# Seven products in place of eight block products for one side of a GRU gate, with VectorE adding partial sums onto a state tile

## The chip, the cores and the metric

The kernel runs on one core of a Trainium2 chip. A core has TensorE (PE, matrix products), VectorE (DVE), ScalarE (ACT), GpSimd (POOL) and SyncE (SP, which issues DMAs here). The engines run their own instruction queues and wait for one another by semaphores. [...] The metric is the device time of one execution in microseconds (us); lower is better.

## What is computed

The input is a batch of 128 graphs with 128 nodes and 256 features per node, and an integer adjacency matrix for each. Four graph layers follow one another, each with a residual and a layer norm: attention by edge type, a message layer, three steps of a gated graph network, and graph attention. The change lies in the third, whose core in the reference is:

```python
for i in range(3):
    m = einsum('bnd,de->bne', h, weight[i])
    aggr = einsum('bst,bsd->btd', A, m)          # A = (adj != 0)
    i_r, i_z, i_n = split(aggr @ w_ih.T + b_ih, 3)
    h_r, h_z, h_n = split(h @ w_hh.T + b_hh, 3)
    r, z = sigmoid(i_r + h_r), sigmoid(i_z + h_z)
    n = tanh(i_n + r * h_n)                      # the candidate
    h = (1 - z) * n + z * h
```

The kernel multiplies `weight[i]` and `w_ih` together once (`c_gi`), so that each step needs the aggregated state, `agT`, times `c_gi`, and the state, `hT`, times `w_hhT`. Everything is fp32, except the sums over neighbours, where the state is split in three bf16 parts.

## The kernel before

**Tiling.** Four graphs form a group, so a state is 256 features by 512 columns (4 graphs x 128 nodes), kept as two tiles of 128 x 512. There are 32 groups. Each passes through `loading`, `layer0`, `layer1`, `gru` and `layer3`; `gru` runs `step` three times. Work of several groups is on the chip at once: a group's three steps are spread over two periods (`SPAN = 2.0`), so the steps of two groups alternate.

**A gate by seven products.** A gate's product is a 256 x 256 weight times a 256 x 512 state, that is, 2 x 2 blocks of 128 x 128 weights and 128 x 256 states. Done directly it takes eight block products. `sums` (line 681) and `gate` (line 703) form it from seven, by Strassen's method in a form with few sums: `sums` adds blocks of the state into a tile (`t_h` for the hidden side, `t_m` for the aggregated side), and the weights' own combinations (`w_sh`, `w_sm`) are made once in `weights` (loop at line 382). In `gate` the four quarters of the result come out of two PSUM banks. The bank `shared` collects products 1, 6, 7 and 4 one after another, and after each of them its running sum is read out into a quarter of the result tile (`snapshot`, by the function `copied` or, at the end, `last`); the next product is added to the same bank only after that read. The bank `other` collects products 2, 5 and 3, and VectorE adds it to the quarters (`added`).

`gate` is called three times in a step:

- `q`: the hidden side of the candidate alone (seven products, one source), with ScalarE reading the shared bank and adding a bias (`hidden`);
- `t_r`: the reset gate, hidden and aggregated side together (fourteen products), ScalarE copying, and `tanh` at the end, since the sigmoid is computed as a tanh of half the argument;
- `t_z`: the update gate, likewise.

The aggregated side of the candidate isn't formed so. `direct` (line 667) takes two products of 512 columns for each half, four in all, into a bank of the tag `ps`. `candidate` (line 757) then computes on VectorE (t + 1) * q in place on the reset tile, adds the bank, and hands it to ScalarE's tanh.

**Buffers.** The PSUM tags `ps` and `gate` have four banks each. The result tiles `t_r`, `t_z`, `q` and the sums `t_m`, `t_h` have one buffer each.

**Order of the work.** Nothing is issued in the order of the program. Every operation is recorded, gets a due time (`nominal`) from `paced` (line 272), in units of `PERIOD`, and a list planner (line 971) issues, on each engine, that operation among those that can start which is due first. It reckons with costs per engine (`dve_cost`, line 249), with delays between engines (`HOP`, `PE_HOP`, `SLACK`) and with free buffers (`start_of`, line 948). It runs when the program is built, so that on the chip each engine has a fixed list. `M_START` and `M_END` set the due times of a step's aggregated part, in periods after the step's start (line 782).

**Layer 3** has a small negation of the softmax's reciprocal sums (`ninv`, line 875) on VectorE.

Of the kernel before, what the change touches and what calls it, by code (L numbers as in the profile page):

```python
# [13 lines left out]
OP = mybir.AluOpType  # L14
# [4 lines left out]
def kernel(  # L19
# [40 lines left out]
    P = 128  # L60
# [5 lines left out]
    NL = weight.shape[0]  # L66
# [69 lines left out]
    def tile_of(tag, shape, bufs=1, dtype=F32, pool=work):  # L136
        buf = Buf(pool, list(shape), dtype, tag, bufs)
        return View(buf, list(shape), [(0, n) for n in shape])

    def bank(tag="ps"):  # L140
        return tile_of(tag, [P, 512], 4, F32, psum)

    FAST = ("tensor_scalar", "tensor_scalar_add", "tensor_scalar_mul")
# [93 lines left out]


    LANDING = 4.2
    HOP = 0.235  # L240
    PE_HOP = 0.55
    SLACK = 0.873

    def pe_cost(op, n, sums):
# [2 lines left out]
    SPLIT = 0.056  # L247

    def dve_cost(op, n, sums):
        return 0.14 + n * (0.00056 if op in FAST else 0.00106)  # L250

    def act_cost(op, n, sums):
        return 0.6 if op == "dma_start" else 0.17 + n * 0.001 + (0.2 if sums else 0.0)
# [3 lines left out]

    PE = Engine("PE", nc.tensor, pe_cost)
    DVE = Engine("DVE", nc.vector, dve_cost)
    ACT = Engine("ACT", nc.scalar, act_cost)  # L260
    POOL = Engine("POOL", nc.gpsimd, pool_cost)
# [1 line left out]
    engines = (PE, DVE, ACT, POOL, SP)  # L263


    PERIOD = 82.744
    SPAN = 2.0
    EAGER, RUSH = 5.34, 0.516
    L0_START, L0_END, L1_START, L1_END, L3_START, L3_END = -2.032, -1.293, -0.75, -0.05, 0.173, 0.919
    H_END, M_START, M_END = 0.179, 0.179, 0.503  # L270

    def paced(start, end, pe_only=False):

# [2 lines left out]
        for op, t in zip(line, took):  # L276
            op.nominal = (start + (end - start) * sofar / total) * PERIOD
            op.urgent = pe_only
# [21 lines left out]
    w_hhT = tile_of("w_hhT", [P, KC, 3 * D])  # L300
    c_gi = tile_of("c_gi", [P, NL, KC, 3 * D])
# [1 line left out]
    w3x = tile_of("w3x", [P, KC, 2 + D])  # L303

    w_sh = tile_of("w_sh", [P, 3, 3, P])
    w_sm = tile_of("w_sm", [P, NL, 3, 2, P])

    def weights():

# [2 lines left out]
        for src, tag, bufs in ((w_ih, "hT", 6), (w_hh, "rest", 4)):  # L312
# [4 lines left out]
            if src is w_ih:  # L317
                for i in range(NL):
                    w = tile_of("hn", [P, KC, D], 3)
# [23 lines left out]
        for n, dst in enumerate((w_ihT, [w_hhT[:, c] for c in range(KC)])):  # L343
            for g in range(NGC // 2):
                nat = nats[n * NGC // 2 + g]
                ps = bank()
# [10 lines left out]
        for i in range(NL):  # L357
            wT = tile_of("h0T", [P, KC, D], 4)
            ps = bank()
# [7 lines left out]
            for d in range(KC):  # L367
                for n0, n1 in ((0, 512), (512, 3 * D)):
                    ps = bank()
                    with PE:  # L370
                        for e in range(KC):
# [4 lines left out]
                                start=(e == 0),  # L376
                                stop=(e == KC - 1),
# [2 lines left out]


        for n in range(NL + 1):
            by, gates = POOL if n > 1 else DVE, 3 if n == 0 else 2
            w = [
                (w_hhT[:, k] if n == 0 else c_gi[:, n - 1, k])[:, : 2 * gates * P].rearrange(
                    "p (g e x) -> p g e x", [P, gates, 2, P], g=gates, e=2
                )
                for k in range(KC)
            ]
            w_s = w_sh if n == 0 else w_sm[:, n - 1]  # L390
            a11, a12, a21, a22 = w[0][:, :, 0], w[1][:, :, 0], w[0][:, :, 1], w[1][:, :, 1]
            s2, s3, s4 = [w_s[:, j] for j in range(3)]
            by.tensor_sub(s3, a11, a21)
            by.tensor_add(a21, a21, a22)
            by.tensor_sub(s2, a21, a11)
            by.tensor_sub(s4, a12, s2)
# [8 lines left out]
        for c in range(KC):  # L405
            for h in range(2):
                DVE.scalar_tensor_tensor(
                    scr, w3x[:, c, 2:], 1.0, arow[:, h * D : (h + 1) * D],
                    op0=OP.mult, op1=OP.mult, accum_out=w3x[:, c, h : h + 1],
# [3 lines left out]
        ps = bank()  # L413
# [229 lines left out]
    def gru(g, s):  # L643
        hT = s.hT
        parts = s.parts
        R, Z, C = 0, KC, 2 * KC
        both = [0, 1]

        def step(i, hT, parts):
            agT, agps = [None] * KC, [None] * KC  # L650
# [13 lines left out]
                agT[c] = tile_of("agT", [P, T], 2)  # L664
                ACT.copy(agT[c], ps)

            def direct(w, v, q, ps=None, of=(0, 1), stop=True):

                start = ps is None
                ps = ps or bank("ps" if q >= C else "gate")  # L670
                with PE:
                    for k in of:
                        PE.matmul(
                            ps, w[:, k, q * P : (q + 1) * P], v[k],
                            start=(start and k == of[0]), stop=(stop and k == of[-1]),
                        )
                return ps

            H = T // 2

            def sums(by, v, w, w_s, src, tag):
# [18 lines left out]

                return of

            def gate(tag, q, sources, copied, added, last=None):

                t = tile_of(tag, [P, 4, H])
                shared, other = bank("gate"), bank("gate")

                def add(cols, p, first=False):  # L710
                    with PE:
                        for k, of in enumerate(sources):
                            PE.matmul(
                                cols, *of(q)[p], start=(first and k == 0),
                                stop=(p in (3, 4) and k == len(sources) - 1), skip_group_check=True,
                            )

                def snapshot(quarter):
                    copied(t[:, quarter], shared[:, :H], quarter // 2)
                    ops[-1].rush = RUSH  # L720

                add(shared[:, :H], 1, True)
                snapshot(0)
                add(other[:, :H], 2, True)
                add(shared[:, :H], 6)
                snapshot(1)
                add(other[:, H:], 5)
                add(shared[:, :H], 7)
                snapshot(3)
                added(t[:, 3], other[:, H:], t[:, 3])  # L730
                if last:
                    last(t[:, 3], t[:, 3], 1)
                add(shared[:, :H], 4)
                (last or copied)(t[:, 2], shared[:, :H], 1)
                add(other[:, H:], 3)
                halves = [t[:, 2 * c : 2 * c + 2].rearrange("p h n -> p (h n)") for c in range(KC)]
                added(halves[0], other, halves[0])
                if last:
                    last(halves[0], halves[0], 0)
                return halves  # L740
# [10 lines left out]
            def tanh(q):  # L751

                return lambda out, in_, c: ACT.activation(
                    out, in_, AF.Tanh, bias=brz[:, q + c : q + c + 1], scale=0.5
                )

            def candidate(c, ps, t, q):
                DVE.scalar_tensor_tensor(t, t, 1.0, q, op0=OP.add, op1=OP.mult)
                DVE.tensor_add(t, t, ps)
                n = tile_of("t_n", [P, T], 2)  # L760
                ACT.activation(n, t, AF.Tanh, bias=bih[:, 2 * KC + c : 2 * KC + c + 1], scale=1.0)
                d = tile_of("t_d", [P, T], 2)
                POOL.tensor_sub(d, hT[c], n)
                return n, d
# [18 lines left out]
            w_i = c_gi[:, i]  # L783
            of_h = sums(POOL, hT, w_hhT, w_sh, hT, "t_h")
            q0, q1 = gate("q", C, (of_h,), hidden, half_more)
            paced(at, at + H_END, True)
            aggregate(0)
            aggregate(1)
            paced(at + M_START - 0.03, at + M_START, True)
            of_m = sums(DVE, agT, w_i, w_sm[:, i], agps, "t_m")  # L790
            t0, t1 = gate("t_r", R, (of_h, of_m), copy, DVE.tensor_add, tanh(R))
            n1, d1 = candidate(1, direct(w_i, agT, C + 1), t1, q1)
            n0, d0 = candidate(0, direct(w_i, agT, C), t0, q0)
            z0, z1 = gate("t_z", Z, (of_h, of_m), copy, DVE.tensor_add, tanh(Z))
            update(1, z1, n1, d1)
            update(0, z0, n0, d0)
# [3 lines left out]
        for i in range(NL):  # L800
            hT, hn, parts = step(i, hT, parts)
# [9 lines left out]
    def layer3(g, s, first, last):  # L811


        n = last - first
# [4 lines left out]
        def tile(tag, shape, bufs=1):  # L819
            tag, bufs = names.get(tag, (tag, bufs))  # L820
            return tile_of(tag, shape, bufs)

        rT = []
        for c in range(KC):
            t = tile("rT", [P, n * N], 2)
# [11 lines left out]
        for b in range(n):  # L837
            ps = bank()
            with PE:
                for c in range(KC):  # L840
                    PE.matmul(
                        ps[:, : 2 + D], rT[c][:, b * N : (b + 1) * N], w3x[:, c, :],
                        start=(c == 0), stop=(c == KC - 1),
# [5 lines left out]
        e = f.rearrange("p (k b) c -> p b k c", [P, n, 4, 32], b=n)  # L849
        if end:  # L850
            ps = bank()
# [19 lines left out]
        pT, rinv = softmax(alpha, three, end, tile)  # L871
# [1 line left out]

        res = tile("xd", [P, n, D])
        ninv = tile_of(f"ninv_{three}", [P, n], 2)
        DVE.tensor_scalar_mul(ninv, rinv, -1.0)
        for h in range(n // 2):
            ps = bank()
            with PE:
# [3 lines left out]
            for j in range(2):  # L883
# [9 lines left out]
                op0=OP.add, op1=OP.add,  # L893
# [54 lines left out]
    def start_of(op):  # L948
# [4 lines left out]
        for buf in op.bufs:  # L953
            if buf.tile is None:
                slot = slot_at(buf)
                if slot is None:
                    return None
                at = max(at, slot + HOP)
                if buf.pool is psum:
# [11 lines left out]
    while left:  # L971
        best = None
        for e in engines:
# [5 lines left out]
            if best is None or at < best[0]:  # L979
                op = min(  # L980
                    (op for t, op in starts if t <= at),
                    key=lambda op: op.nominal - (EAGER if op.urgent and e is not PE else 0.0) - op.rush,
                )
                best = (at, op)
        at, op = best
        e = op.engine
# [12 lines left out]
        for other in op.after.values():  # L999
            other.waiting -= 1  # L1000
            hop = 0.0 if other.engine is e and not op.landing else SLACK if not other.urgent else HOP
            if hop == HOP and other.engine is PE:
                hop = PE_HOP
            other.ready = max(other.ready, end + hop)
# [31 lines left out]
```

## Time and profile before

| | |
|---|---|
| median of 3 runs | 2764.72 us (2764.5 to 2765.69) |
| profiled execution | 2763.69 us, its span 2761.8 us |
| mean granted TensorE clock | 0.991 |
| busy PE, DVE, POOL, ACT | 2702.3, 2304.1, 1666.2, 1584.2 us |
| DMA | 321.88 MB, mean 117 GB/s |

Every instruction is recorded by one helper, so all have one line (L232) and are told apart by their tiles: `gate<-t_m,c_gi` is a product of the aggregated side's sums with the combined weights into a bank of the tag `gate`, `ps<-agT,c_gi` a direct product of the candidate. PE is TensorE's products, PEld its weight loads. An fp32 product shows as two matmul instructions (x2). In a row of groups, the columns after the bar are busy time, mean ns of one, and the idle time before them with what ended it. In a row of waits they are total us, times, and the longest. In a timeline they are start and duration in us. Busy time of TensorE counts overlapped ends of matmuls, so that the distance between starts says more than durations.

### The profile page before, as it was taken

Reading aid. Unit: us, or ns where it says so; the run is one execution under the profiler, and the core shown is the slowest. Engines: PE = TensorE matmul, PEld = TensorE weight load, DVE = VectorE, ACT = ScalarE, POOL = GpSimd, SP = SyncE. Lnnn points to the kernel's source line nnn. Section 1 sums busy time; section 2 is a strip of 40 time slices with the busy share of each in tenths; the row PEclk is TensorE's granted clock in tenths of the full one; section 3 lists DMA queues with packets and bytes.
Section 4 is the critical chain, followed back from the end, with each engine's and each line's share of the span. In section 5 each row is a group of like instructions: output and inputs, shape, how many; then the busy total and the mean of one; then the engine's idle time right before and its main releaser. Section 6 shows DMA issues by size and latency. Waiting matters only on the chain.

```text
span 2761.8 us, 44048 instructions
## 1 busy us (share of the span) xinstructions
PE 2702.3 (98%) x13756; PEld 2138.1 (77%) x13756; DVE 2304.1 (83%) x5108; ACT 1584.2 (57%) x3704; POOL 1666.2 (60%) x1606
## 2 busy tenths in 40 slices
PE   8899999999999999999999999999999999999996
PEld 5677787887887887887887887887887887787774
DVE  5787888888888888888888888888888898888875
ACT  4454665555665655665655665655665655665554
POOL 4544666655666655666655666655676655675542
PEclk9999999999999999999999999999999999999996
DMA  5545555555555556555655556655556555545441
GB/s 121 129 90 99 115 126 129 120 109 124 122 125 131 121 108 129 118 124 133 121 107 127 121 121 134 121 110 123 121 121 134 124 109 120 116 110 118 99 88 43
DMA packets 1397130, 321.88 MB, mean 117 GB/s; under 512 B 1142560, under 2 KB 1388448, under 8 KB 1396896
## 3 DMA queue, kind: packets, MB, share of 16 engines
q1 hardware_dynamic: 1394448, 316.69, 53.7%
q10 hardware_dynamic: 2448, 2.36, 0.3%
q8 instruction: 111, 1.82, 0.3%
q14 instruction: 123, 1.01, 0.1%
HBM read 185.74 MB, written 133.15 MB: 115 GB/s over the span
## 4 chain that ended last, share of the span: by engine, by line
PE 94%; DVE 3%; POOL 1%; ACT 1%; DMA 1%; issue 1%; ACTq 0%; POOLq 0%; DVEq 0%; SPq 0%
PE gate L232 52%; PE ps L232 42%; DVE t_r L232 0%; POOL t_h L232 0%; DVE xb L232 0%; DVE st L232 0%; DMA rest<-in_L_gnn_w_hh_dram 0%; DVE z L232 0%; POOL rstd L232 0%; DMA hn<-in_L_gnn_weight_dram 0%; POOL xa L232 0%; DVE xa L232 0%; DVE t_d L232 0%; POOL t_d L232 0%; DVE hT L232 0%
## 5 line engine op out<-in xcount | busy, mean ns | idle before, releaser
L232 ACT ACTIVATE q<-gate,bhn 128x256 f32<-128x256 f32 x384 | 183.0, 477 | 314.4 <-PE gate L232 313.1
L232 PE MATMUL ps<-agT,c_gi 128*128 128x512 f32 x768 | 356.0, 592 | 0.0
L232 PE MATMUL gate<-t_h,w_hhT 128*128 128x256 f32 x1152 | 345.2, 381 | 5.7 <-ACT t_z L232 4.3
L232 PE MATMUL gate<-t_h,w_sh 128*128 128x256 f32 x1152 | 337.1, 383 | 4.2 <-ACT q L232 1.7
L232 POOL TENSOR_TENSOR rstd<-rstd,neg_half 128x4 f32<-128x4 f32 (+1 forms) x128 | 142.4, 1112 | 218.2 <-DVE rstd L232 215.1
L232 PEld LDWEIGHTS gate<-t_h,w_sh 128*128 128x128 f32 x1152 | 213.7, 191 | 62.8 <-issue 30.4
L232 PEld LDWEIGHTS ps<-xs,xT 128*128 128x128 f32 x2048 | 249.7, 193 | 11.5 <-ACT xs L232 2.6
L232 PEld LDWEIGHTS gate<-t_h,w_hhT 128*128 128x128 f32 x1152 | 211.7, 191 | 56.1 <-issue 16.3
L232 PE MATMUL ps<-xs,xT 128*128 128x128 f32 x2048 | 251.8, 276 | 2.2 <-ACT xs L232 1.3
L232 ACT COPY t_z<-gate 128x256 f32<-128x256 f32 x288 | 107.1, 372 | 244.6 <-PE gate L232 244.0
L232 PE MATMUL ps<-w_um,x1T 128*128 128x512 f32 x512 | 237.1, 595 | 0.2 <-ACT x1T L232 0.2
L232 PEld LDWEIGHTS ps<-agT,c_gi 128*128 128x128 f32 x768 | 145.8, 190 | 114.5 <-issue 106.0
L232 PE MATMUL gate<-agT,c_gi 128*128 128x256 f32 x768 | 229.2, 380 | 2.6 <-ACT agT L232 2.6
L232 PE MATMUL gate<-t_m,c_gi 128*128 128x256 f32 x768 | 228.5, 379 | 0.0
L232 PE MATMUL gate<-t_m,w_sm 128*128 128x256 f32 x768 | 228.4, 379 | 0.0
L232 PE MATMUL gate<-hT,w_hhT 128*128 128x256 f32 x768 | 222.8, 385 | 5.6 <-DVE hT L232 5.6
L232 POOL TENSOR_SCALAR mk<-a_f 128x512 uint8<-128x512 f32 x128 | 201.3, 1579 | 12.2 <-DVE alpha L232 6.6
L232 ACT ACTIVATE xs<-xT,acol 128x512 f32<-128x512 f32 x256 | 182.1, 717 | 40.9 <-PE ps L232 31.5
L232 POOL MEMSET hu<- 128x1 f32 x128 | 10.3, 96 | 303.8 <-DVE fac L232 224.5
L232 DVE TENSOR_TENSOR t_z<-gate,t_z 128x256 f32<-128x256 f32 x192 | 104.2, 543 | 101.4 <-ACT t_z L232 53.7
L232 POOL TENSOR_TENSOR t_d<-h0T,t_n 128x512 f32<-128x512 f32 x64 | 82.9, 1295 | 174.0 <-ACT t_n L232 171.1
L232 PEld LDWEIGHTS gate<-hT,w_hhT 128*128 128x128 f32 x768 | 141.8, 191 | 48.1 <-issue 23.6
(197 smaller groups left out, 7280.1 us busy)
## 6 DMA issues: line engine op xcount, KB each, us to landing
way_h<-z SPq DMA_DIRECT2D x190, 256.0 KB, 2.4
hn<-way_h SPq DMA_DIRECT2D x760, 64.0 KB, 2.4
way<-z SPq DMA_DIRECT2D x126, 256.0 KB, 3.2
x_blocks<-in_x_dram SPq DMA_DIRECT2D x256, 64.0 KB, 2.3
x_in<-in_x_dram SPq DMA_DIRECT2D x32, 512.0 KB, 3.8
way_x<-xb SPq DMA_DIRECT2D x32, 512.0 KB, 2.9
way_p<-z SPq DMA_DIRECT2D x62, 256.0 KB, 2.6
probT<-way_p SPq DMA_DIRECT2D x248, 64.0 KB, 2.3
```

Of the source, the lines that this page charges most:

```text
L232: getattr(self.engine, name)(*[a.real() if isinstance(a, View) else a for a in args], **{k: a.real() if isinstance(a, View) else a for k, ...
```

## The change

The aggregated side of the candidate goes through `gate` as a fourth call. It has one source (`of_m`), and in place of copies it has `onto`: VectorE adds the shared bank's running sum onto the quarter of the reset tile, which by then holds (t + 1) * q. There is no result tile of its own: `whole` turns the reset gate's half back into a view of its whole buffer. `direct` goes. Both (t + 1) * q operations are recorded ahead of the gate, first half first. The weight combinations are made for three gates in place of two for `c_gi` too (`w_sm` grows), and `ninv` goes to ScalarE. The planner's costs, delays, period and due times are changed.

```diff
-    HOP = 0.235
-    PE_HOP = 0.55
+    HOP = 0.217
+    PE_HOP = 0.441
...
-        return 0.14 + n * (0.00056 if op in FAST else 0.00106)
+        return 0.095 + n * (0.00056 if op in FAST else 0.00106) + (0.08 if sums else 0.0)
...
-    PERIOD = 82.744
+    PERIOD = 82.004
...
-    L0_START, L0_END, L1_START, L1_END, L3_START, L3_END = -2.032, -1.293, -0.75, -0.05, 0.173, 0.919
-    H_END, M_START, M_END = 0.179, 0.179, 0.503
+    L0_START, L0_END, L1_START, L1_END, L3_START, L3_END = -1.947, -1.293, -0.7, -0.05, 0.168, 0.874
+    H_END, M_START, M_END = 0.179, 0.12, 0.503
...
-    w_sm = tile_of("w_sm", [P, NL, 3, 2, P])
+    w_sm = tile_of("w_sm", [P, NL, 3, 3, P])
...
-            by, gates = POOL if n > 1 else DVE, 3 if n == 0 else 2
+            by = POOL if n > 1 else DVE
             w = [
-                (w_hhT[:, k] if n == 0 else c_gi[:, n - 1, k])[:, : 2 * gates * P].rearrange(
-                    "p (g e x) -> p g e x", [P, gates, 2, P], g=gates, e=2
+                (w_hhT[:, k] if n == 0 else c_gi[:, n - 1, k]).rearrange(
+                    "p (g e x) -> p g e x", [P, 3, 2, P], g=3, e=2
                 )
...
-            def direct(w, v, q, ps=None, of=(0, 1), stop=True):
...
+            def whole(t):
+                return View(t.buf, t.buf.shape, [(0, n) for n in t.buf.shape])
+
+            def onto(out, in_, c):
+                DVE.tensor_add(out, in_, out)
+
             def gate(tag, q, sources, copied, added, last=None):
...
-                t = tile_of(tag, [P, 4, H])
+                t = tile_of(tag, [P, 4, H]) if isinstance(tag, str) else whole(tag)
...
-                if last:
+                if last not in (None, onto):
                     last(t[:, 3], t[:, 3], 1)
                 add(shared[:, :H], 4)
                 (last or copied)(t[:, 2], shared[:, :H], 1)
                 add(other[:, H:], 3)
+                if copied is onto:
+                    added(t[:, :2].rearrange("p h n -> p (h n)"), other, t[:, :2].rearrange("p h n -> p (h n)"))
+                    return None
...
-            def candidate(c, ps, t, q):
-                DVE.scalar_tensor_tensor(t, t, 1.0, q, op0=OP.add, op1=OP.mult)
-                DVE.tensor_add(t, t, ps)
+            def candidate(c, t):
...
-            n1, d1 = candidate(1, direct(w_i, agT, C + 1), t1, q1)
-            n0, d0 = candidate(0, direct(w_i, agT, C), t0, q0)
+            for t, q in ((t0, q0), (t1, q1)):
+                DVE.scalar_tensor_tensor(t, t, 1.0, q, op0=OP.add, op1=OP.mult)
+            gate(t0, C, (of_m,), onto, DVE.tensor_add, onto)
+            n1, d1 = candidate(1, t1)
+            n0, d0 = candidate(0, t0)
...
-        DVE.tensor_scalar_mul(ninv, rinv, -1.0)
+        ACT.mul(ninv, rinv, -1.0)
```

More of the change, by code (lines that the diff above doesn't have):

```diff
@@ L665, in aggregate @@
                 ACT.copy(agT[c], ps)
-            def direct(w, v, q, ps=None, of=(0, 1), stop=True):
[L669 to L677, printed above, removed]
             H = T // 2
```

## The prediction

> **What bounds the kernel now.** I read the head of the page first, then the busy table over one period, then TensorE's waits.
>
> ```profile
> span 2761.8 us, 44048 instructions
> PE 2702.3 (98%) x13756; PEld 2138.1 (77%) x13756; DVE 2304.1 (83%) x5108; ACT 1584.2 (57%) x3704; POOL 1666.2 (60%) x1606
> PE 94%; DVE 3%; POOL 1%; ACT 1%; DMA 1%; issue 1%; ACTq 0%; POOLq 0%; DVEq 0%; SPq 0%
> ```
>
> TensorE (PE) is busy for 98% of the span, and 94% of the chain that ended last lies on it. The same POOL instruction on successive groups starts at 600.13, 682.79 and 765.47 us: a period of 82.67. The stretch table for one such period, 1400 to 1482.67 us, and TensorE's waits from 200 to 2500 us:
>
> ```profile
> core 0: us, PE busy (x) PEld busy (x) DVE busy (x) ACT busy (x) POOL busy (x), PEclk, DMA share, GB/s
> ...
> sum 82.67, PE 82.67 PEld 66.01 DVE 71.29 ACT 49.12 POOL 52.43; mean PE 27.56 PEld 22.00 DVE 23.76 ACT 16.37 POOL 17.48
> ```
>
> ```profile
> PE gate L232 <- POOL t_h L232: 0.8, 2, 0.6
> PE gate L232 <- ACT t_z L232: 0.5, 1, 0.5
> ```
>
> In 2300 us TensorE waited 1.3 us. VectorE (DVE) is next, 71.29 of 82.67 us (86%). Busy time of overlapped matmuls can flatter, so I take pitches (start to start) from the timeline of TensorE:
>
> ```profile
> 1430.01 0.59 PE L232 MATMUL gate<-hT,w_hhT 128*128 128x256 f32 x2
> ...
> 1433.03 0.59 PE L232 MATMUL gate<-t_m,w_sm 128*128 128x256 f32 x2
> ...
> 1451.87 3.60 PE L232 MATMUL ps<-agT,c_gi 128*128 128x512 f32 x8
> 1455.30 0.59 PE L232 MATMUL gate<-hT,w_hhT 128*128 128x256 f32 x2
> ```
>
> From 1430.01 to 1433.03 lie seven products of 256 columns: 3.02 us, 0.43 each. The candidate's four direct products of 512 columns take 1455.30 - 1451.87 = 3.43 us. There is no gap in either.
>
> [...] So each sum read out of an open bank is a round: product, read, next product. [...] The trace agrees on rounds (the waits above end with an evictor) and shows VectorE waiting for gate products. [...] the trace has 417 and 668, which I use.
>
> **The change, part by part.**
>
> *Products.* Per step 3.43 us goes and 7 x 0.43 = 3.02 comes: -0.41 us. Weight loads rise from 8 to 14 of 190 ns, two in each 0.43 us pitch, as the existing gates have them: hidden. Some 29 of the 32 periods lie where TensorE is full (200 to 2600 us), 87 of 96 steps: -35.7. The other nine I count half: -1.8. Sum -37.5 us.
>
> *VectorE.* The groups by shape:
>
> ```profile
> L232 DVE TENSOR_TENSOR t_r<-t_r,ps 128x512 f32<-128x512 f32 x192 | 131.4, 684 | 8.3 <-PE ps L232 0.6 <-PE gate L232 0.5
> L232 DVE TENSOR_TENSOR t_z<-gate,t_z 128x512 f32<-128x512 f32 x96 | 64.2, 668 | 47.6 <-PE gate L232 47.5
> L232 DVE TENSOR_TENSOR t_z<-gate,t_z 128x256 f32<-128x256 f32 x96 | 40.1, 417 | 53.7 <-ACT t_z L232 53.7
> ```
>
> Two adds of 684 ns go; five of 417 and one of 668 come: 2.75 - 1.37 = +1.39 us a step, +4.2 a period. The negation of rinv leaves VectorE (median 665 ns, once a group). So 71.29 + 4.2 - 0.7 = 74.8 of about 82 us: 91%. That costs nothing by itself while TensorE has 81 us to do. Were that cover gone, every microsecond of it would lengthen the period.
>
> *Rounds.* The candidate gains four rounds a step on its shared bank (384 in all), with one product each, so other work must fill them. The hidden-side gate already runs this shape with ScalarE as reader, and all gates already have one VectorE read between two products of `other`; TensorE's 1.3 us above is what they cost. Uncovered rounds elsewhere stop TensorE for 0.46, 0.51, 0.56 us (around 2590 to 2720 us). Bounds: none uncovered, 0; every one, 384 x 0.5 = 192 us. I choose one in twenty, 19 x 0.5 = +9.6 us, because VectorE's queue is fuller than ScalarE's (57%) and because work in the `ps` banks, which TensorE does meanwhile, falls by those 3.43 us a step.
>
> *Reset state held longer.* `t_r` has one buffer. ScalarE's timeline:
>
> ```profile
> 1420.15 0.38 ACT L232 COPY t_r<-gate 128x256 f32<-128x256 f32 x1
> ...
> 1440.43 0.71 ACT L232 ACTIVATE t_n<-t_r,bih 128x512 f32<-128x512 f32 x1
> ...
> 1444.90 0.38 ACT L232 COPY t_r<-gate 128x256 f32<-128x256 f32 x1
> ```
>
> It is held from its first copy to the last tanh that reads it: 21.0, 19.6 and 19.7 us in this period, mean 20.1 of the 27.56 that each of three steps has. The one add (0.68) before that tanh becomes first add, three rounds and last add. A two-source round of the last update gate, with nothing in the way, took 1.66 us (copies at 2718.25 and 2719.91); less one product 0.54 that is 1.12. So 0.42 + 3 x 1.12 + 0.1 + 0.67 = 4.6, or +3.9 a step: 24.0 of about 27.3. It fits. The queued waits behind VectorE's adds are the other gates' adds, `t_m` and the state update, which release TensorE.
>
> *ScalarE* gets 33 small negations. The nearest row, a one-column read of the accumulator, takes 191 ns: 6.3 us, within its idle 43%. Bounds 0 and, on the path, 6.3; I take 0. *Setup*: the combinations of the weights grow from 256 to 384 columns. On POOL eight operations of 0.72 us at 27 to 42 us grow by at most half, +2.9 us; behind them wait the masks of the first group. On VectorE four grow by 0.14. Their first users start after 79 us. Bounds 0 to 3.4, I take +0.5. *Banks*: the candidate leaves `ps` for two of the four `gate` banks. From first read to last, gates hold pairs for some 116 of 2 x 82.67 us now, and three more of about 10 us make 146: still below. *End*: in the last step the direct products delay the reset gate (2708.57 to 2712.00); that 3.4 us goes, 3.9 comes, and the update gate's rounds run beside it: bounds -3 to +6, I take +1.5. *Planner*: its costs and due times change, and so the order on every queue, the DMA issues on SP's too (DMA share 0.55). It issues whichever startable operation is due first and never holds TensorE back until a due time, so no direct cost; bounds -5 to +20, in the range.
>
> Sum: -37.5 + 9.6 + 0.5 + 1.5 = -25.9. The profiled execution took 2763.7 (span 2761.8 and 1.9 around it), so 2737.8; the median shown stands 1.0 above it: about 2738.
>
> **The rivals.** *Full gain*: TensorE stays as gapless as now. For it: twelve rounds a step cost nothing today. Against: VectorE at 91%. -37.5 + 2 gives 2729. *VectorE's waits take most*: now it idles 82.67 - 71.29 = 11.4 us a period, nearly all waits for others (9.5 us in the larger rows from 400 to 2400 us). With 74.8 busy, the waits must fall below 7.9 before anything is won. If they stop at 7.6, the period is 82.4: 0.27 x 29 = 8 us won, 2757. *No change*: the same at 7.9, or the product saving eaten by 0.4 us of gaps a step: 2765. *Slower*: the single `t_r`. If the candidate's rounds run no faster than the hidden gate's do under load (1440.06 to 1451.04, 11 us from first read to last), the hold grows by more than the 27.56 - 20.1 - 0.4 = 7.1 us a step that is free, 0.4 being a handover; from there it sets the period. At +7.5 it is 3 x 28.0 = 84.0 us: +1.3 x 29 = 38, so 2803. Against it: a candidate product that is late is due first on TensorE, so it tends towards the unloaded 3.9.
>
> **How the numbers follow.** Forecast 0.52 (2730 to 2750), full gain 0.20 (2723 to 2732), VectorE's waits 0.12 (2750 to 2759), no change 0.04, slower 0.12. About 0.2% (5.5 us) is what a measurement tells from no change. Faster is 0.52 + 0.20 + 0.12 = 0.84, same 0.04, slower 0.12. The range 2724 to 2758 holds the forecast, most of the full gain and most of the third case: about 0.8. The forecast's own is 2730 to 2750.
>
> **What would show it.** Right: a period near 81.7 (82.67 - 1.24 + 0.3), 1344 more gate matmuls (two to a product) and none of 512 columns into `ps` from `agT`, VectorE near 75 us a period, TensorE's waits of 0.1 us a step, ended by VectorE adds on `t_r`. Wrong: a period of 82.6 or more with TensorE idle before gate products, or the gap between last read and next copy of `t_r` at its minimum in every step.

## The result and the profile after

The changed kernel takes 2846.29 us (2845.3 to 2847.98), the kernel before 2764.76: a ratio of 1.0295 (1.0277 to 1.0313), 81.5 us slower, where 2738 was forecast. The three lines of the page of the changed kernel that answer to those shown of before, and the costliest group of its page:

```profile
span 2843.4 us, 45272 instructions
PE 2706.4 (95%) x14332; PEld 2232.4 (79%) x14332; DVE 2393.1 (84%) x5459; ACT 1590.6 (56%) x3737; POOL 1658.0 (58%) x1606
PE 63%; DVE 27%; DMA 3%; issue 2%; ACT 2%; POOL 1%; SPq 1%; ACTq 0%; POOLq 0%; DVEq 0%
...
L232 DVE TENSOR_TENSOR t_r<-gate,t_r 128x256 f32<-128x256 f32 (+1 forms) x768 | 368.3, 485 | 206.4 <-PE gate L232 191.6
```

TensorE's share of the chain fell from 94% to 63%, and VectorE's rose from 3% to 27%: TensorE no longer runs through, it hands the end back and forth with VectorE. The granted clock is the same (0.992 and 0.991). The cast on POOL that marks a group starts at 782.22 us and, eighteen groups later, at 2325.70: a mean period of 85.75 us where it was 82.67. From some 440 us on the casts come 84.4 and 87.2 us apart in turn, so the pattern repeats every second group; before, each came 82.7 after the last. From the sixth cast to the last the changed kernel takes 75.3 us longer, most of the 81.5. The stretch table over those eighteen periods (busy time by engine, with instruction counts):

```profile
782.22:2325.70 1543.48, 1493.09 (x7994) 1242.97 (x7992) 1333.45 (x3043) 886.58 (x2088) 935.24 (x901) 1.00 0.56 117
```

TensorE, the first engine of the row, stands idle for 50.4 us of 1543, or 2.80 a period, in place of nothing (more of its starts are late by too little to show as idle; the section on why the prediction was wrong sums them up). VectorE (the third) is busy for 1333.45 / 18 = 74.1 us a period, close to the 74.8 forecast. So it isn't full. TensorE's waits from 200 to 2500 us of the changed kernel (total us, times, longest):

```profile
PE gate L232 <- DVE t_r L232: 29.4, 53, 1.0
PE gate L232 <- DVE t_z L232: 22.7, 25, 1.5
PE gate L232 <- DVE q L232: 18.2, 38, 0.7
PE gate L232 <- ACT q L232: 1.8, 1, 1.8
```

Before, all waits of this stretch came to 1.3 us. Now three reads by VectorE hold TensorE for 70.3 us. The groups of TensorE in the same stretch tell which products stood behind them (last column: idle before, by what it was ended):

```profile
L232 PE MATMUL gate<-t_m,c_gi 128*128 128x256 f32 x966 | 284.4, 381 | 6.8 <-DVE t_r L232 6.8
L232 PE MATMUL gate<-agT,c_gi 128*128 128x256 f32 x969 | 282.1, 382 | 9.5 <-DVE q L232 9.5
L232 PE MATMUL gate<-t_m,w_sm 128*128 128x256 f32 x964 | 279.1, 382 | 10.5 <-DVE t_r L232 10.5
L232 PE MATMUL gate<-hT,w_hhT 128*128 128x256 f32 x642 | 192.7, 387 | 19.7 <-DVE t_z L232 19.3 <-DVE t_r L232 0.2
...
L232 PE MATMUL gate<-hT,w_sh 128*128 128x256 f32 x324 | 101.8, 396 | 20.6 <-DVE t_r L232 11.9 <-DVE q L232 8.7
```

The candidate's aggregated side uses only the first three kinds (and `agT,w_sm`, which has no idle time), with 26.8 us together. In the gates with two sources each such product follows its hidden-side partner on the same bank, and the partner takes the wait; so by the sequence on TensorE all 26.8 us are the candidate's: 9.5 before its first product, for a bank that the gate `q` still held, and 17.3 in its own rounds. The two hidden-side rows, none of whose products the change touched, have 40.3 us: 19.7 before products that open a gate, nearly all of it behind a read of `t_z`, and 20.6 in the rounds of the gates `t_r` and `q`. These gates ran without such waits before. A wait of this sort in detail, first TensorE's, then ScalarE's and VectorE's timeline of the changed kernel (start, duration):

```profile
1413.59 0.59 PE L232 MATMUL gate<-t_m,c_gi 128*128 128x256 f32 x2
1415.10 0.70 PE L232 MATMUL gate<-hT,w_sh 128*128 128x256 f32 x2 [0.91 <-DVE t_r L232]
```

```profile
1411.64 0.37 ACT L232 COPY t_r<-gate 128x256 f32<-128x256 f32 x1 [1.49 <-PE gate L232]
```

```profile
1412.04 0.70 DVE L232 COPY_PREDICATED alpha<-mk,ps 128x512 f32<-128x512 uint8 x1
1412.63 0.67 DVE L232 SCALAR_TENSOR_TENSOR xd<-ps,xd 128x512 f32<-128x512 f32 x1
1413.34 0.43 DVE L232 BATCH_NORM_STATS2 st<-xd 128x6 f32<-128x256 f32 x1
...
1414.55 0.17 DVE L232 TENSOR_SCALAR rstd<-mv 128x4 f32<-128x4 f32 x1
1414.62 0.42 DVE L232 TENSOR_TENSOR t_r<-gate,t_r 128x256 f32<-128x256 f32 x1
```

The product at 1415.10 belongs to a reset gate and adds to the bank that the add at 1414.62 reads. The add had what it needed when ScalarE's copy ended at 1412.01. VectorE was at work without a stop, on statistics and updates of another stage for which TensorE wasn't waiting, and the add stood behind them for 2.6 us. In the trace of the change, TensorE, VectorE, ScalarE and POOL start their 14332, 5459, 3737 and 1606 instructions in the sequence of the lists that the planner made, as the tiles that they write tell; so they do in the trace of before. The six runs below that keep the planner's order have the lists of the kernel that each was made from (two additions a step more in one of them), and their times differ from it by up to 26 us. With both lists fixed, this read, 2.6 us late, costs TensorE 0.9 us.

### The profile page after: what moved, and what is told of

It reads as the page before. It is cut to its first block, busy times and chain, and to the rows that moved or that the text cites. A ratio compares the mean times of both kernels' runs of the same rounds, so it can differ in the third digit from the quotient of the medians.

```text
span 2843.4 us, 45272 instructions
## 1 busy us (share of the span) xinstructions
PE 2706.4 (95%) x14332; PEld 2232.4 (79%) x14332; DVE 2393.1 (84%) x5459; ACT 1590.6 (56%) x3737; POOL 1658.0 (58%) x1606
## 4 chain that ended last, share of the span: by engine, by line
PE 63%; DVE 27%; DMA 3%; issue 2%; ACT 2%; POOL 1%; SPq 1%; ACTq 0%; POOLq 0%; DVEq 0%
PE gate L232 43%; PE ps L232 21%; DVE t_r L232 4%; DVE st L232 2%; DVE z L232 2%; DVE t_m L232 2%; DVE hT L232 2%; DVE rest L232 2%; DVE t_z L232 2%; DVE q L232 2%; DVE t_d L232 1%; DVE xa L232 1%; DVE xb L232 1%; DVE mv L232 1%; DVE alpha L232 1%
## 5 line engine op out<-in xcount | busy, mean ns | idle before, releaser
L232 DVE TENSOR_TENSOR t_r<-gate,t_r 128x256 f32<-128x256 f32 (+1 forms) x768 | 368.3, 485 | 206.4 <-PE gate L232 191.6
L232 PE MATMUL gate<-t_m,c_gi 128*128 128x256 f32 x1152 | 338.7, 381 | 8.6 <-DVE t_r L232 8.4
L232 PE MATMUL gate<-agT,c_gi 128*128 128x256 f32 x1152 | 336.4, 382 | 10.4 <-DVE q L232 10.2
L232 PE MATMUL gate<-t_m,w_sm 128*128 128x256 f32 x1152 | 332.7, 382 | 10.9 <-DVE t_r L232 10.7
L232 PEld LDWEIGHTS gate<-t_h,w_hhT 128*128 128x128 f32 x1152 | 213.0, 190 | 71.8 <-issue 32.4
L232 PE MATMUL gate<-hT,w_hhT 128*128 128x256 f32 x768 | 232.9, 390 | 29.6 <-DVE t_z L232 19.3
L232 PEld LDWEIGHTS gate<-agT,c_gi 128*128 128x128 f32 x1152 | 216.6, 190 | 48.5 <-DVE q L232 18.6
L232 PEld LDWEIGHTS gate<-t_m,w_sm 128*128 128x128 f32 x1152 | 216.3, 190 | 48.8 <-DVE t_r L232 19.6
L232 PEld LDWEIGHTS gate<-t_m,c_gi 128*128 128x128 f32 x1152 | 216.4, 190 | 44.3 <-DVE t_r L232 14.9
L232 POOL TENSOR_TENSOR t_d<-hT,t_n 128x512 f32<-128x512 f32 x128 | 171.1, 1358 | 105.0 <-ACT t_n L232 104.9
L232 ACT ACTIVATE t_r<-t_r,brz 128x256 f32<-128x256 f32 x192 | 118.1, 615 | 203.7 <-DVE t_r L232 166.1
L232 POOL TENSOR_TENSOR t_h<-hT 128x256 f32<-128x256 f32 x128 | 97.8, 785 | 197.8 <-PE gate L232 192.4
```

The lines of the kernel that those rows point to most:

```text
L232: getattr(self.engine, name)(*[a.real() if isinstance(a, View) else a for a in args], **{k: a.real() if isinstance(a, View) else a for k, ...
```

## The experiments

The question: does the work of the change cost the time (the candidate's rounds, the hold of `t_r`, VectorE's load, the banks), or the order in which the planner lists it? Each expectation names the theories it tells apart. Six kernels keep the order of every queue as it was and change one thing in it; this is said with each.

**The change's figures on the old work.** The direct candidate comes back into the changed kernel; the planner's new costs and due times and `ninv` on ScalarE stay.

```diff
-            gate(t0, C, (of_m,), onto, DVE.tensor_add, onto)
-            n1, d1 = candidate(1, t1)
-            n0, d0 = candidate(0, t0)
+            n1, d1 = candidate(1, direct(w_i, agT, C + 1), t1, q1)
+            n0, d0 = candidate(0, direct(w_i, agT, C), t0, q0)
```

> The changed kernel with the candidate's aggregated side put back to four direct products (and the weight combinations with it); the planner's new constants and the negation on ScalarE stay. If the new constants make a bad order for any work, most of the 81.5 us stays: 2820 or more. If the loss comes from the seven products (rounds, VectorE's load, or the reset state's hold), it goes: 2755 to 2785.

2829.37 us, 1.0236 (1.0206 to 1.0266) of before: slow without a single product of the change. Its TensorE waits from 200 to 2500 us:

```profile
PE gate L232 <- ACT t_z L232: 32.8, 32, 2.1
PE gate L232 <- DVE t_z L232: 4.0, 9, 0.5
```

The kernel before waited 0.5 us for ScalarE's copies into `t_z`, this one 32.8. The copies are the same; their place is new. (The mean granted clock was 0.988, against 0.992 of the kernel before beside it. By estimate that is at most 0.4%, 11 us, of the 66.)

**The old figures on the new work.** The changed kernel with all of the planner's costs and due times of before.

```diff
-    HOP = 0.217
-    PE_HOP = 0.441
+    HOP = 0.235
+    PE_HOP = 0.55
...
-    PERIOD = 82.004
+    PERIOD = 82.744
...
-    H_END, M_START, M_END = 0.179, 0.12, 0.503
+    H_END, M_START, M_END = 0.179, 0.179, 0.503
```

> The changed kernel's work with all of the planner's constants from the kernel before (delays, VectorE's cost, period, due times). If the new constants are what loses the time: 2730 to 2780. If the work itself is harder to order, the new constants help it, and this is slower than the changed kernel: 2870 or more.

2850.1 us, 1.0308 (1.0278 to 1.0338): as slow as the change. So neither part alone is the culprit. New figures on old work cost 66 us, old figures on new work 84, both new 82.

**VectorE's load on the order of before.** Two additions of 128x512 to a scratch tile in each step, on the kernel before with its order kept.

```diff
+                DVE.tensor_add(tile_of("dm", [P, T]), hT[0], hT[1])
+                ops[-1].took, ops[-1].waits, ops[-1].holds = 0.0, False, False
```

> The kernel before, every queue in the same order, with two further VectorE adds of 128x512 a step, written to a scratch tile that nobody reads: 2 x 0.69 = 1.4 us a step, what the change adds on VectorE, without a single new wait between engines. The output stays as it was. If VectorE's load by itself makes its queue late: 2810 or more. If it is the new rounds, the constants or the hold: 2765 to 2780.

2776.49 us, 1.0046 (1.0026 to 1.0065), and TensorE's waits are hardly more than before:

```profile
PE gate L232 <- POOL t_h L232: 1.4, 1, 1.4
PE gate L232 <- ACT t_z L232: 0.5, 1, 0.5
PE gate L232 <- DVE q L232: 0.2, 1, 0.2
```

From cast to cast over eighteen groups, VectorE is busy for 1362 of 1491 us (91%), more than in the change, and TensorE has no idle time:

```profile
773.33:2264.77 1491.44, 1491.44 (x7670) 1186.41 (x7669) 1362.42 (x2953) 874.55 (x2070) 990.68 (x901) 1.00 0.57 122
```

An extra load of this size costs 13 us in an order that fits, and not 82.

**Less for VectorE in the order of the change.** First, other work on VectorE is taken out: the third part of the split into bf16 is left out, so the values it stood for are too coarse. By the trace this takes 2.3 us a period off VectorE (74.1 to 71.8), less than the 3.8 that were expected.

```diff
-                    split_up[c] = split(turning[c], DVE)
+                    rest = tile_of("rest", [P, G, P], 4)
+                    DVE.tensor_sub(rest, turning[c], turning[c].high())
+                    DVE.tensor_sub(rest.half(0)[:, 0:1, :32], rest[:, 0:1, :32], rest.high()[:, 0:1, :32])
+                    split_up[c] = turning[c].high(), rest.high(), rest.high()
```

> The changed kernel, every queue in the same order, rounds untouched, but other VectorE work cut by about as much as the change adds: the second subtraction of each state split (mean 1.07 us, four a group) covers 32 columns in place of 512, and the neighbour sums take the second part twice, so the third bf16 part of the state is left out. About 3.8 us a period less on VectorE. If its load causes the loss: 2760 to 2785. If the rounds do, or the hold: 2815 or more.

Second, the candidate's adds are cut to a third of their columns (the sums of the other columns are left out), which brings VectorE's load back to about that of before.

```diff
             def onto(out, in_, c):
-                DVE.tensor_add(out, in_, out)
+                DVE.tensor_add(out[:, :84], in_[:, :84], out[:, :84])
```

> The changed kernel, every queue in the same order, every wait of the candidate's rounds kept, but VectorE's six adds of the candidate's gate cover 84 columns in place of 256 and 168 in place of 512, so that they take about what the two adds before took (1.37 us a step); the other columns of the sums are left out of the output. If VectorE's load is the cause: 2760 to 2790. If it is the waits at fixed places in the queues: 2810 or more; the cut of 3.8 us elsewhere gave 2826, so that in between would be 2815 to 2830.

2826.32 (1.0225, 1.0195 to 1.0255) and 2820.51 us (1.0201, 1.0171 to 1.0231). Both give back some: 20 and 26 us of 82. With VectorE's load as before (2284.9 us busy against 2304.1), 55 us of loss remain, and the waits with it:

```profile
PE gate L232 <- DVE t_z L232: 18.7, 23, 1.4
PE gate L232 <- DVE t_r L232: 18.7, 39, 0.9
PE gate L232 <- DVE q L232: 15.8, 26, 0.7
```

**The candidate's rounds.** In the order of the change, the three adds between the candidate's products read a tile in SBUF in place of the shared bank, so the next product needn't wait for them. What they should have added is left out. The fourth round, in which VectorE reads the bank `other` before the last product adds to it, stays.

```diff
-                    copied(t[:, quarter], shared[:, :H], quarter // 2)
+                    (unread if copied is onto else copied)(t[:, quarter], shared[:, :H], quarter // 2)
```

> The changed kernel, every queue in the same order, but the three adds in the middle of the candidate's gate read a tile of the aggregated state in SBUF and not the shared bank: same operation, same place in the queue, no wait between product, add and next product. The running sums of the candidate are left out of the output by this. If the rounds cause the loss: 2740 to 2790. If VectorE's load, the constants or the single reset tile cause it: 2820 or more.

2855.03 us, 1.0329 (1.0299 to 1.0359): nothing is won. The candidate's middle products no longer wait, but its last one, `agT,w_sm`, which had no idle time in the change, now does. TensorE's groups and waits from 200 to 2500 us:

```profile
L232 PE MATMUL gate<-t_m,c_gi 128*128 128x256 f32 x960 | 283.1, 381 | 0.0
L232 PE MATMUL gate<-t_m,w_sm 128*128 128x256 f32 x960 | 275.0, 379 | 0.0
L232 PE MATMUL gate<-agT,w_sm 128*128 128x256 f32 x482 | 145.5, 384 | 21.9 <-DVE t_r L232 21.9
```

```profile
PE gate L232 <- DVE t_r L232: 33.9, 28, 2.1
PE gate L232 <- DVE t_z L232: 28.9, 25, 2.1
PE gate L232 <- DVE q L232: 15.5, 27, 0.7
```

TensorE comes to the fourth round sooner, and VectorE's read of `other`, at its old place in the list, doesn't. So three rounds of four can go without a gain while the list stays; what the candidate would cost without any round isn't shown. The 9 us above the change are no finding: the mean granted clock was 0.988 in this profiled execution and 0.992 in the change's, which by estimate is worth up to 0.4%, 11 us.

**The hold of the reset state.** In the order of the change, `t_r` gets a second buffer (room for it comes from the `st` tiles, two for four).

```diff
-                t = tile_of(tag, [P, 4, H]) if isinstance(tag, str) else whole(tag)
+                t = tile_of(tag, [P, 4, H], 2 if tag == "t_r" else 1) if isinstance(tag, str) else whole(tag)
```

> The changed kernel, every queue in the same order, with a second buffer for the reset tile t_r (room for it comes from two buffers in place of four for the small statistics tiles). If the single reset tile is what sets the period, as the slower rival of the prediction has it: 2745 to 2785. If not: 2835 to 2850.

2844.71 us, 1.0289 (1.0259 to 1.0318), with the waits at 28.5, 22.6 and 18.1 us: no difference. The prediction's rival "slower" falls, as far as its mechanism goes.

**The banks.** The planner reckons with a bank for every PSUM tile (all 14332 matmuls in the trace of the change write to one, 8064 to the tag `gate` and 6268 to `ps`), the one that came free first; the allocator of the program hands them out by its own rule. In the order of the change, each tile gets the bank that the planner reckoned with.

```diff
-                self.tile = self.pool.tile(self.shape, self.dtype, tag=self.tag, name=self.tag, bufs=self.bufs)
+                tag, bufs = (self.tag, self.bufs) if self.pool is not psum else (f"{self.tag}{self.slot}", 1)
+                self.tile = self.pool.tile(self.shape, self.dtype, tag=tag, name=self.tag, bufs=bufs)
```

> The changed kernel, every queue in the same order, each PSUM tile in the bank that the planner had in mind for it (one tag for each bank), where otherwise the choice among four is left to the allocator. If TensorE's waits for a bank that was read late come from a bank other than the planned one: 20 to 35 us less than the changed kernel, 2810 to 2826. If the planned banks are as late: 2840 to 2850.

2826.98 us, 1.0224 (1.0195 to 1.0254): 19 us come back, nearly all from one of the three waits.

```profile
PE gate L233 <- DVE t_r L233: 29.0, 53, 1.0
PE gate L233 <- DVE q L233: 20.7, 38, 0.7
PE gate L233 <- DVE t_z L233: 3.4, 12, 0.3
```

So the wait on `t_z` (22.7 us) was one for a bank, behind the last read of an update gate, where by the planner's reckoning another bank was free earlier.

**Other orders for the same work.** No single cost explains the loss, so the last question is put directly: is there an order in which the change's own work runs without waits? The planner's figures were moved together, by a search that replays each order's queues with durations from the profile. The first kernel has the work of the change unaltered, the banks of the planner, and the candidate's two sums in banks of the tag `ps`, as the direct candidate had.

```diff
-    HOP = 0.217
-    PE_HOP = 0.441
-    SLACK = 0.873
+    HOP = 0.235
+    PE_HOP = 0.596
+    SLACK = 0.896
...
-        return 0.095 + n * (0.00056 if op in FAST else 0.00106) + (0.08 if sums else 0.0)
+        return 0.126 + n * (0.00056 if op in FAST else 0.00106) + (0.08 if sums else 0.0)
...
-    PERIOD = 82.004
+    PERIOD = 83.682
...
-    EAGER, RUSH = 5.34, 0.516
-    L0_START, L0_END, L1_START, L1_END, L3_START, L3_END = -1.947, -1.293, -0.7, -0.05, 0.168, 0.874
-    H_END, M_START, M_END = 0.179, 0.12, 0.503
+    EAGER, RUSH = 4.49, 0.414
+    L0_START, L0_END, L1_START, L1_END, L3_START, L3_END = -2.032, -1.294, -0.750, -0.050, 0.173, 0.919
+    H_END, M_START, M_END = 0.178, 0.133, 0.503
...
-                shared, other = bank("gate"), bank("gate")
+                of_c = copied is onto or tag == "t_c"
+                shared, other = (bank("ps"), bank("ps")) if of_c else (bank("gate"), bank("gate"))
```

> The change's own work, unaltered (seven products, VectorE's adds onto the reset state, ninv on ScalarE), in another fixed order: the planner's figures are moved (a wait for TensorE priced 0.596 instead of 0.441, an add of VectorE 0.126 instead of 0.095, period 83.68 instead of 82.00, the layers' due times shifted by some hundredths of a period), each PSUM tile stays in the bank that the planner gave it, and the candidate's two sums take banks of the group that the direct candidate used instead of the gates' group. Theory O (the order, not the work, loses the time: reads of VectorE stand too late in its queue): a better order gives back at least half of the 82 us, so 2765 to 2805, period 82.3 to 83.6, and TensorE's waits for VectorE fall from 3.7 us a period to under 1.5. Rival W (the seven products and their adds cost this time in whatever order, as VectorE is too full): 2820 or more, as with the banks of the planner alone (2827), and waits of 3 us a period.

2758.46 us (2756.07 to 2761.29), 0.998 (0.9972 to 0.9989) of before: 88 us faster than the change, and a little faster than the kernel before. Page, stretch table over nineteen periods and TensorE's waits from 200 to 2500 us:

```profile
span 2759.5 us, 45499 instructions
PE 2686.8 (97%) x14332; PEld 2249.7 (82%) x14332; DVE 2377.1 (86%) x5459; ACT 1585.2 (57%) x3737; POOL 1645.5 (60%) x1606
PE 85%; DVE 9%; DMA 2%; POOL 2%; issue 1%; ACT 1%; SPq 0%; ACTq 0%; DVEq 0%; POOLq 0%
```

```profile
765.60:2330.30 1564.70, 1561.21 (x8438) 1319.66 (x8437) 1399.58 (x3212) 932.71 (x2205) 978.27 (x950) 1.00 0.59 122
```

```profile
PE ps L233 <- DVE fac L233: 2.1, 14, 0.2
PE gate L233 <- POOL t_h L233: 0.5, 1, 0.5
PE gate L233 <- DVE t_z L233: 0.2, 1, 0.2
```

The counts of instructions on each engine are those of the change to the last one (14332, 5459, 3737, 1606), and so they are for each operation with its tiles and shape, but for the tag of the candidate's banks. VectorE is busy for a larger share of the time (1399.58 of 1564.70, 89.4%, against 86.4%), and yet TensorE waits 2.8 us in place of 72. The period is 1564.70 / 19 = 82.35 us.

The next control takes the two edits to banks without the new figures.

```diff
-    HOP = 0.235
-    PE_HOP = 0.596
-    SLACK = 0.896
+    HOP = 0.217
+    PE_HOP = 0.441
+    SLACK = 0.873
```

(against the kernel of 2758 us; all other figures likewise as the change has them)

> The changed kernel with the planner's banks and the candidate's two sums in the direct candidate's group of banks, both as in o_ap (2758), but with all of the planner's figures as the change has them. It differs from x_banks (2827) by the group alone and from o_ap by the figures alone. Theory G (the gates' four banks are what the candidate ran short of): most of o_ap's gain comes from the group, so 2775 or less. Theory O (the figures make the order, and an order fits one set of waits): the group alone changes the order at random, 2800 to 2850, and o_ap's gain is the figures'.

2844.49 us, 1.0293 (1.0276 to 1.031). The group of banks by itself wins nothing; it is 17 us behind the kernel with the planner's banks alone. From the kernel of 2758 us it differs in nothing but the planner's figures, and so in the order: that alone is 86 us. (The figures without the edits to banks weren't run.)

Two more orders have another reader for the candidate: ScalarE copies the shared bank into a tile `t_c` (room for it comes from the `st` tiles), VectorE completes that tile and adds it to the reset state. In the first its sums take `ps` banks, in the second `gate` banks; each has figures of its own, the first for instance `PE_HOP = 0.651` and `PERIOD = 82.849`.

```diff
-            gate(t0, C, (of_m,), onto, DVE.tensor_add, onto)
+            c0, c1 = gate("t_c", C, (of_m,), copy, DVE.tensor_add)
+            for t, c in ((t1, c1), (t0, c0)):
+                DVE.tensor_add(t, t, c)
```

> The seven products kept, but their reader changed: ScalarE makes the candidate's two copies into a tile of their own (t_c, half-precision of nothing, same float32), VectorE adds the products to that tile and then t_c onto the reset state (two adds of 128x512 more a step, no read-modify-write on t_r from PSUM), in an order of its own, with the planner's banks and the candidate's sums in the direct candidate's group of banks. Theory O: with seven products TensorE has 1.24 us a period less work than before, so with an order that leaves it no waits this runs below the kernel before: 2725 to 2760, period 81.5 to 82.5. Rival W: VectorE's extra work shows in any order: 2790 or more.

> As o_sp (ScalarE reads the shared half of the candidate's sums into a tile t_c), but the candidate's sums stay in the gates' group of banks as in the change, in an order of its own. Theory O with the banks as a cause of their own: slower than o_sp by 5 to 20 us, since sixteen more tiles a period ask for four banks; 2740 to 2775. Theory O without the banks: the same as o_sp within 4 us. Rival W: 2790 or more.

2744.66 us, 0.993 (0.9915 to 0.9945), and 2754.34 us, 0.9965 (0.9952 to 0.9978). The first is the fastest kernel of this study, 20.1 us below the kernel before and 101.6 below the change. Over nineteen periods of it:

```profile
765.30:2323.90 1558.60, 1551.19 (x8437) 1321.29 (x8436) 1433.13 (x3098) 1007.78 (x2432) 1019.14 (x951) 1.00 0.58 123
```

The period is 82.03 us, and VectorE is busy for 92% of it (1433.13 of 1558.60). The second differs from it in its order as well as its banks, so the 10 us between them aren't a price of the banks. No kernel with the work of before and newly searched figures is among the runs, so how much of the 20 us is due to the seven products, and how much to the search, isn't shown.

## Why the prediction was wrong, step by step

- **What bounds the kernel**: right for the kernel before. But that TensorE ran without a gap was a property of that order, and the prediction took it for one of the work.
- **Products, -0.41 us a step**: the size is right. There are 576 more matmuls, which is 1344 more of 256 columns less 768 of 512. From 600 to 2300 us the median distance between the starts of matmuls of 256 columns is 0.216 us before, after, and in the kernel of 2758 us, two to a product, and 0.429 for 512 columns. But of 1.24 us a period that kernel kept 0.32 (with 0.18 of idle time, (1564.70 - 1561.21) / 19) and the fastest 0.64 (with 0.39). The rest is in starts that are late by less than shows as idle: a product's modelled end lies 0.59 - 0.43 = 0.16 us past the normal start of the next, so a wait below that is invisible. Summed over all matmuls from 600 to 2300 us, the distance to the next start beyond the median for the shape comes to 0.28 us a period before, 1.18 in the kernel of 2758 us, 0.84 in the fastest and 4.53 in the change. Over the kernel before that is 0.90, 0.57 and 4.25, which is what their periods lack of the full saving: 0.92, 0.60 and 1.24 + 3.08 = 4.32. So, by this sum, the saving was there in the changed kernel too, and late starts took it and 3.08 us more.
- **VectorE, 74.8 us a period, "costs nothing by itself"**: the size is right (74.1). The claim holds nearly in an order that fits (13 us for more load than this, with VectorE 91% busy; 89% and 92% in the kernels of 2758 and 2745 us) and not in the order of the change, where less load is worth 20 to 26 us.
- **Rounds, 19 uncovered of 384, +9.6 us**: too few, but a small part of the miss. From 200 to 2500 us 39 of the candidate's rounds were uncovered, 17.3 us. (Three of its four rounds are on the shared bank, the fourth is on `other`. And of the 1.3 us of waits that the prediction took for the price of all rounds today, 0.8 were for POOL's sums `t_h`, and not for a read.) What the step overlooked is the rest of the list. The *other* gates' rounds lost their cover, 20.6 us, and so did the change of banks between gates: 19.7 us before other gates' first products, 9.5 before the candidate's.
- **Reset state held, 24.0 us**: six holds from 1408.55 to 1567.35 us took 17.5, 29.0, 19.3, 20.3, 22.6 and 24.8 us, a mean of 22.3, with 2.2 to 8.9 us between the last read and the next copy. It fits, as said, and a second buffer changes nothing.
- **Banks, "still below"**: wrong for this order. 19 us went on banks that were handed out while others were free earlier by the planner's reckoning.
- **Planner, "no direct cost; bounds -5 to +20"**: this is the step that failed. Its argument, that the planner issues what is due first and never holds TensorE back, is about the planner's own reckoning when the program is built. On the chip the lists are fixed, and each engine waits at the head of its list for whatever the reckoning had wrong (TensorE 0.91 us in the wait at 1415.10, for a read 2.6 us late). The same work took 2846 us in one order and 2758 in another, and with the banks handed out by the same rule the figures alone made 86 us of difference. So the term reaches to some 90 us, and it was bounded by 20.
- **The rivals**: "VectorE's waits take most" had the right place, TensorE waiting for VectorE, but bounded it by how full VectorE can get. At 89.4% it held nothing up, so fullness wasn't the limit; and nothing in that rival let the waits exceed the saving. The full gain of 2729 wasn't reached by any order tried. (A slip in the forecast's own sum: 2737.8 and 1.0 are 2738.8, and not 2738.)
- **Range and chances**: the first sign of "wrong" came, a period of 85.75 us with TensorE idle before gate products; the second, a reset state with no room left, did not. 12 in 100 for slower rested on the single `t_r` alone, and it was the wrong mechanism. The full list of slower ways should have held "a new order loses the fit". A hint lay in the diff: the new price of an add of 256 columns is 0.095 + 256 x 0.00106 = 0.37 us, the trace of before has 0.417, and the old price was 0.41. That this price alone is the cause isn't shown (with the old price, too, the new work took 2850 us).

What stays open is which figure does the harm. The runs show only that five pairs of work and figures ended between 2827 and 2850 us (old work with new figures, new work with old ones, with the change's, and these with other banks twice), and four others between 2745 and 2765 (the kernel before and the three whose figures were searched for).

## What to carry to other kernels

Where queues are fixed by a planner when the program is built, price an edit to its figures, or to the work it plans, as a new order, and not at nothing: the hidden waits of all the other work are at stake, here about 80 us of 2765. Before the work of a change is blamed, search for an order that fits it and look at the waits; the same instructions went from 2846 to 2758 us. To say what the work itself is worth, search as long for the work of before; no such run is in this study. And hand out the buffers as the planner reckoned: that gave 19 us back. That costs taken from the trace would have helped as well isn't shown.

## What the runs showed that was not expected

- VectorE can be busy for 89 to 92% of the time while TensorE's waits show 2.8 us (at 89%), 2.1 (at 91%) and 11.3 (at 92%) of 2300; at 86% in another order TensorE waited 72 us. Its share says little on whether it holds TensorE up.
- Taking away waits at one place moved them on: with three of the candidate's rounds gone, 17.3 us of waits became 21.9 at the fourth, and those on `t_z` rose from 22.7 to 28.9 us.
- A view of idle time shows only part of what TensorE loses. From 600 to 2300 us of the change, starts were late by 89.8 us in all, and 54.5 of them show as idle; before, it was 5.7 and none.
- Fourteen weight loads in place of eight a step cost TensorE nothing that the distance of starts shows: the median stays at 0.216 us a matmul in all three kernels.
